# Mask or bias and row maximum in one VectorE instruction per head and block, in a two-layer transformer kernel

## The chip, the cores and the metric

The kernel runs on one core of one Trainium2 chip. The metric is the device time of one execution in microseconds (us). Five engines work side by side, each through its own queue in order: TensorE (PE, with PEld for its weight loads), VectorE (DVE), ScalarE (ACT), GpSimd (POOL) and SyncE (SP, which issues transfers).

## The reference

Two layers of different kinds run over 8 x 256 tokens of width 128, in float32. Each block is followed by a residual and a layer normalisation.

```python
x = _layernorm(x + attn0(x))   # 16 heads of 64, softmax(q k^T * scale) v, no mask
x = _layernorm(x + ffn0(x))    # tiles chosen by signatures, splines
x = _layernorm(x + attn1(x))   # linear attention gated with window attention
x = _layernorm(x + ffn1(x))    # causal attention, then 8 soft experts
```

Two of them have scores with something added to them ahead of the softmax. In the window attention, each query sees the 65 keys around it, with a learned bias per offset and head:

```python
s = einsum('bhsd,bhsd->bhs', qh, ks) * scale + rel_bias[off + WINDOW]
s = where(0 <= pos + off < S, s, -inf);  attn = softmax(s)      # 16 heads of 8
```

In the causal attention of the last block (16 heads of 64), queries and keys are normalised to length 1 first:

```python
q = l2norm(q) * q_scale;  k = l2norm(k) * k_scale
logits = where(causal, einsum('bhid,bhjd->bhij', q, k) * 10.0, NEG_INF)
attn = softmax(logits)
```

## The kernel before, in words

The tokens are cut into eight groups of 512 (two sequences each). Every group goes through five stages: A (attention without mask), B (the first feed-forward block), C (linear and window attention), D (causal attention) and E (the experts). Stages of different groups run at the same time, so that at any moment several of them share the engines.

The order of the work is not written by hand. Each piece of work is a task added by `W.add(engine, cost, function, ...)`, with a cost in nanoseconds, the buffers that it reads and writes, and a due time. `Plan.order` then makes one list out of all the tasks: it takes in turn the task that can begin first, by these costs, and counts the buffers of each class (`SLOTS`) as they are taken and given back. Tasks marked "VS" or "SV" may go to VectorE or ScalarE; the planner picks the one that would start it sooner. The queues of the engines hold the instructions in that order, whatever the chip then does. A changed cost can therefore change the order on all engines.

The scores of an attention live in two PSUM buffers of class "s" (1024 columns each), which stages A, B, C and D share. A buffer is used so:

- `scores` on TensorE writes the scores.
- `top` on VectorE adds the mask or bias, if there is one, and finds the maximum of each row, negated, into a small buffer `nmx` (class "m").
- `weigh` on ScalarE computes the exponentials out of it (L623, in stage C L1065), with `nmx` as its bias. Then the buffer is free for the next scores.

In stages A and D the function `pair` does this for two heads and one sequence of 256 tokens; there are 128 such pairs in each of the two stages. In stage A `top` is one maximum over 1024 columns (L606). In stage D the queries are cut into two halves of 128: the first half needs 128 keys, the second 256, so each head has 384 columns. There `top` adds a mask of 128x128 (`cmask`) to the two diagonal blocks of both heads (L597, 512 columns), takes the maxima (L602, two instructions), and multiplies them by the scale of the row, `rq` (L604).

Stage C works on blocks of 64 queries with 16 heads laid out as 8 slots of two heads each; a block sees 96 keys at the ends of a sequence and 128 within it. There are 64 blocks, 32 of each kind. There `top` adds `band`, the bias laid out per slot, to all 8 slots by one instruction (L1053), and takes the 8 maxima by another (L1054).

Other lines that matter below: L514 is every matrix multiplication, L651 the transposition of the weights, L636 their division by the sum on GpSimd, L520 and L522 are copies out of PSUM on ScalarE and VectorE (tasks that either may take), L536 is a step of the layer normalisation on GpSimd, L1020 prepares the queries of a block of stage C on GpSimd. Stage C takes its tiles of 512 columns from class "c", of which there are nine.

Of the kernel before, what the change touches and what calls it, by code (L numbers as in the profile page):

```python
# [12 lines left out]
ALU = mybir.AluOpType  # L13
AX = mybir.AxisListType
# [3 lines left out]
P = 128  # L18
# [13 lines left out]
NEG = -1.0e30  # L32
# [15 lines left out]
    ("k1", 256, 5),  # L48
    ("b", 512, 2),
    ("sc", 288, 1),  # L50
    ("c", 512, 9),
    ("qm", 512, 2),
    ("pbC", 512, 2),
    ("ptC", 512, 2),
# [183 lines left out]
def kernel(ctx: ExitStack, tc: tile.TileContext, a: dict, out: bass.AP):  # L238
    nc = tc.nc
# [7 lines left out]
    def ctile(name, shape, dtype=F32):  # L247
        return const.tile(shape, dtype, name=name, tag=name)
# [7 lines left out]
    W = Plan(slots)  # L256
# [171 lines left out]
    band = ctile("band", [P, WH // 2, P])  # L428
# [6 lines left out]
    def setup_c():  # L435
# [34 lines left out]
        out=hm, in_=hm, compare_op=ALU.is_ge, fill=0.0, base=0, pattern=[[-WD, WH]], channel_multiplier=1  # L470
    )
    nc.gpsimd.affine_select(
        out=hm, in_=hm, compare_op=ALU.is_ge, fill=0.0, base=WD - 1, pattern=[[WD, WH]], channel_multiplier=-1
# [14 lines left out]
    nc.gpsimd.memset(blk2, 0.0)  # L488
    nc.gpsimd.memset(blk2[:DH, 0:1], 1.0)
    nc.gpsimd.memset(blk2[DH:, 1:2], 1.0)  # L490
    cmask = ctile("cmask", [P, P])
    make_causal_mask(nc, cmask, NEG)
    ones1 = ctile("ones1", [P, 1])
    nc.gpsimd.memset(ones1, 1.0)

# [5 lines left out]
    def pe(n, cols=P, count=1, passes=2):  # L501
        return count * passes * max(0.84 * n, 0.87 * cols)

    def dve(n, count=1):
        return count * (60 + 1.05 * n)

    def scl(n, count=1):
        return count * (60 + 0.84 * n)
# [4 lines left out]
    def mm(o, lhsT, rhs, start=True, stop=True):  # L513
        nc.tensor.matmul(o, lhsT=lhsT, rhs=rhs, start=start, stop=stop)  # L514
# [3 lines left out]
    def copy(e, o, i):  # L518
        if e == "S":
            nc.scalar.copy(o, i)  # L520
        else:
            nc.vector.tensor_copy(o, i)  # L522

    def layernorm(o, z, name, after=()):

# [42 lines left out]
    def pair(pi, qT, kT, v, ov, causal, rq):  # L568

        chain = chain_d if causal else chain_a
        ncol = 3 * P if causal else 4 * P


        col = {0: (2 * P, P), 1: (0, 2 * P)} if causal else {0: (0, 2 * P), 1: (2 * P, 2 * P)}
        sps = W.buf("s", "sps")
        nmx, sums = W.buf("m", "nmx"), W.buf("m", "sums")
        S2 = "p (a k) -> p a k"

        def scores():
            q, k, s = qT("p (i t) -> p i t", t=S), kT("p (i t) -> p i t", t=S), sps(S2, a=2)
            for qc in range(2):
                c0, nk = col[qc]

                for par in range(2):
                    r = slice(par * DH, (par + 1) * DH)
                    mm(s[:, par, c0 : c0 + nk], q[r, pi, qc * P : (qc + 1) * P], k[r, pi, :nk])

        W.add("P", pe(ncol, cols=0), scores, r=[qT, kT], w=[sps, chain[0]], mode="r")  # L590

        def top():
            s = sps(S2, a=2)
            n = nmx(n=4, pattern="p (a b) -> p a b", a=2)
            if causal:
                diag = s[:, :, P : 3 * P].rearrange("p a (b k) -> p a b k", k=P)
                nc.vector.tensor_tensor(  # L597
                    out=diag, in0=diag, in1=cmask.unsqueeze(1).unsqueeze(1).to_broadcast([P, 2, 2, P]), op=ALU.add
                )
                for qc in range(2):  # L600
                    c0, nk = col[qc]
                    nc.vector.tensor_reduce(n[:, :, qc], s[:, :, c0 : c0 + nk], AX.X, ALU.max, negate=True)  # L602
                rqp = rq("p (b h) -> p h b", n=8, b=2)[:, 2 * pi : 2 * pi + 2, :]
                nc.vector.tensor_tensor(out=n, in0=n, in1=rqp, op=ALU.mult)  # L604
            else:
                nc.vector.tensor_reduce(n, s.rearrange("p a (b k) -> p a b k", k=S), AX.X, ALU.max, negate=True)  # L606

        cost = 1790 if causal else dve(1024)
        W.add("V", cost, top, r=[rq] if causal else [], w=[sps, nmx])

        pts = []
        for par in range(2):
            pb, pt = W.buf("pb", "pb"), W.buf("pt", "pt")
            sm = (sums, par)

            def weigh(par=par, pb=pb):
                s = sps(S2, a=2)
                for qc in range(2):
                    c0, nk = col[qc]
                    kw = {}  # L620
                    if causal:
                        kw["scale"] = rq()[:, qc * 4 + 2 * pi + par : qc * 4 + 2 * pi + par + 1]
                    act(  # L623
                        pb()[:, c0 : c0 + nk], s[:, par, c0 : c0 + nk], AF.Exp,
                        bias=nmx()[:, 2 * par + qc : 2 * par + qc + 1],
                        accum_out=sums()[:, 2 * par + qc : 2 * par + qc + 1], **kw,
                    )

            W.add("S", 976 if causal else 900, weigh, r=[nmx, (sps, par)] + ([rq] if causal else []), w=[pb, sm], table="exp")
            W.add("V", 73, lambda par=par: nc.vector.reciprocal(sums()[:, 2 * par : 2 * par + 2], sums()[:, 2 * par : 2 * par + 2]), w=[sm])  # L630

            def norm(e, par=par, pb=pb):
                for qc in range(2):
                    c0, nk = col[qc]
                    eng = nc.gpsimd if e == "G" else nc.vector
                    eng.tensor_scalar(  # L636
                        pb()[:, c0 : c0 + nk], pb()[:, c0 : c0 + nk],
                        sums()[:, 2 * par + qc : 2 * par + qc + 1], 1.0, ALU.mult, ALU.mult,
                    )

            W.add("G", (802 if causal else 910,), lambda norm=norm: norm("G"), r=[sm], w=[pb])
            tps = W.buf("p", "tps")

            def turn(pb=pb, tps=tps):

                at = 0
                for kc in range(2):
                    for qc in range(2):
                        c0, nk = col[qc]
                        if kc * P < nk:  # L650
                            nc.tensor.transpose(  # L651
                                tps()[:, at * P : (at + 1) * P], pb()[:, c0 + kc * P : c0 + (kc + 1) * P], ident
                            )
                            at += 1

            W.add("P", pe(P, count=ncol // P, passes=1), turn, r=[pb], w=[tps, chain[1]], hold=[pt])
            W.add("VS", (dve(ncol), scl(ncol)), lambda e, pt=pt, tps=tps: copy(e, pt()[:, :ncol], tps()[:, :ncol]), r=[tps], w=[pt])
            pts.append(pt)
        ops = W.buf("p", "ops")

        def values():
            vv = v("p (k n) -> p k n", k=2)
            for kc in range(2):
                q0 = P if causal and kc else 0
                for par in range(2):
                    hc = slice((2 * pi + par) * DH, (2 * pi + par + 1) * DH)
                    mm(
                        ops()[par * DH : (par + 1) * DH, q0:S],
                        vv[:, kc, hc],
                        pts[par]()[:, kc * S : kc * S + S - q0],  # L670
                        start=kc == 0,
                        stop=kc == 1,
                    )

        W.add("P", pe(ncol, cols=0), values, r=[v] + pts, w=[ops, chain[2]], hold=[ov], mode="c64")
        W.add("VS", (dve(256), scl(256)), lambda e: copy(e, ov(), ops()[:, :S]), r=[ops], w=[ov])

    def into_width(ovs, w, hf, o, name):
# [14 lines left out]
    def stage_a(g):  # L693
# [12 lines left out]
        def unit(b, p2):  # L706
# [31 lines left out]
            for i in range(2):  # L738
                W.at = base + (4 * b + p2 + (i + 1) / 3) / 8
                ov = W.buf("ov", "ovA")  # L740
                pair(i, qT, kT, v, ov, False, None)
                got.append(ov)
# [181 lines left out]
    def stage_c(g):  # L924
        xx = xg[g]
        V, G, A = nc.vector, nc.gpsimd, nc.scalar
# [46 lines left out]
        for b in range(2):  # L973
# [37 lines left out]
            for i, (w0, w1_) in enumerate(win_of):  # L1011
                W.at = base + 0.1 + 0.4 * b + 0.09 * i
                nk = w1_ - w0
                t0 = w0 - (QC * i - HALF)
                c0 = b * S + QC * i
# [23 lines left out]
                sps = W.buf("s", "spsC")  # L1039
# [9 lines left out]
                nmx = W.buf("m", "nmxC")  # L1049

                def top(sps=sps, nmx=nmx, nk=nk, t0=t0):
                    s8 = sps("p (u k) -> p u k", u=8)[:, :, :nk]
                    V.tensor_tensor(out=s8, in0=s8, in1=band[:, :, t0 : t0 + nk], op=ALU.add)  # L1053
                    V.tensor_reduce(nmx()[:, :8], s8, AX.X, ALU.max, negate=True)  # L1054

                W.add("V", 130 + 2 * dve(8 * nk), top, w=[sps, nmx])
                pts = []
                for half in range(2):
                    pb, pt, tps = W.buf("pbC", "pbC"), W.buf("ptC", "ptC"), W.buf("p", "tpsC")
# [318 lines left out]
```

## Time and profile before

| | |
|---|---|
| median of 3 runs | 2264.16 us (2259.54 to 2265.47) |
| profiled execution | 2259.16 us, its span 2257.3 us |
| TensorE busy | 2126.6 us, 94% of the span |
| VectorE busy | 1711.4 us, 76% |
| ScalarE busy | 1316.0 us, 58% |
| GpSimd busy | 801.7 us, 36% |
| granted TensorE clock, mean | 0.982 of full speed |

A line of the groups reads: line, engine, operation, what it writes <- what it reads, their shapes and count, then busy time in us and the mean of one in ns, then the idle time of that engine just before these instructions and who ended it. A line of the waits reads: who waited for whom, us in total, times, longest. A line of the timeline reads: start, length, instruction. The records of neighbouring instructions on one engine can overlap, so the distance between two starts is what an instruction costs its queue.

### The profile page before, as it was taken

What the parts mean: (1) busy time and instruction counts of PE and PEld (TensorE: products, weight loads), DVE (VectorE), ACT (ScalarE), POOL (GpSimd) and SP (SyncE); (2) the same over time, 40 slices, a digit from 0 to 9 for tenths busy, and PEclk for the clock granted to TensorE, in tenths of its full rate; (3) what the DMA queues carried; (4) which work ended last, traced back from release to release, by engine and by line L of the source; (5) the groups of instructions that cost most, each with busy time, mean ns of one, the idle gap of its engine ahead of it and who ended that gap; (6) DMA issues with size and microseconds to landing.
All of it is one profiled execution on the core that took longest, in us unless ns stands there. A gap on an engine that the chain in (4) does not pass through costs nothing.

```text
span 2257.3 us, 50085 instructions
## 1 busy us (share of the span) xinstructions
PE 2126.6 (94%) x18474; PEld 1611.8 (71%) x18474; DVE 1711.4 (76%) x5167; ACT 1316.0 (58%) x3824; POOL 801.7 (36%) x1441
## 2 busy tenths in 40 slices
PE   6999999999999999999999999999899989989987
PEld 5777767777777677776777767777667767767755
DVE  4789898888678977688767897588876976785741
ACT  3556656666466656565565666565565645654642
POOL 6435352444143531335213352143521441330421
PEclk8999999999999999999999999999999999999998
DMA  6100000000100001100010000100011001001101
GB/s 149 24 1 2 2 1 1 2 2 20 43 16 11 2 15 38 34 1 2 15 47 20 2 1 25 48 11 2 1 38 39 7 19 37 22 7 51 29 20 42
DMA packets 61029, 47.98 MB, mean 21 GB/s; under 512 B 4609, under 2 KB 51297, under 8 KB 60785
## 3 DMA queue, kind: packets, MB, share of 16 engines
q1 hardware_dynamic: 59200, 43.09, 6.8%
q8 instruction: 146, 2.39, 0.5%
q0 software_dynamic: 1008, 0.65, 0.3%
q10 hardware_dynamic: 576, 1.05, 0.2%
q14 instruction: 99, 0.80, 0.1%
HBM read 41.89 MB, written 2.88 MB: 20 GB/s over the span
## 4 chain that ended last, share of the span: by engine, by line
PE 31%; DVE 16%; ACT 3%; issue 2%; POOL 1%; POOLq 0%; DVEq 0%; ACTq 0%
PE p L514 25%; PE p L651 2%; PE s L514 2%; DVE m L602 2%; DVE s L597 1%; ACT pb L623 1%; DVE m L606 1%; DVE m L531 1%; POOL pb L636 1%; DVE s L1053 1%; DVE m L1054 1%; PE p L1071 1%; DVE m L1147 1%; DVE pt L522 1%; DVE m L1149 1%
## 5 line engine op out<-in xcount | busy, mean ns | idle before, releaser
L636 POOL TENSOR_SCALAR pb<-pb,m 128x256 f32<-128x256 f32 (+1 forms) x1024 | 452.4, 458 | 710.6 <-DVE m L630 611.2
L1309 ACT ACTIVATE hid<-p,b 128x512 f32<-128x512 f32 x256 | 169.3, 688 | 285.3 <-PE p L514 283.8
L651 PE MATMUL p<-ident,pb 128*128 128x128 f32 x1792 | 293.8, 284 | 22.4 <-POOL pb L636 17.0
L623 ACT ACTIVATE pb<-s,m 128x256 f32<-128x256 f32 x512 | 239.0, 488 | 112.5 <-DVE m L606 100.9
L623 ACT ACTIVATE pb<-s,m,m 128x128 f32<-128x128 f32 (+1 forms) x512 | 257.7, 525 | 62.3 <-DVE m L604 47.7
L651 PEld LDWEIGHTS p<-ident,pb 128*128 128x128 f32 x1792 | 208.1, 143 | 113.6 <-POOL pb L636 66.0
L514 PE MATMUL p<-h,we 128*128 128x512 f32 x512 | 251.5, 624 | 2.9 <-ACT hid L1309 2.5
L514 PEld LDWEIGHTS p<-we,hid 128*128 128x128 f32 x2048 | 238.6, 192 | 15.6 <-issue 10.0
L514 PE MATMUL p<-we,hid 128*128 128x128 f32 x2048 | 246.9, 276 | 1.0 <-ACT hid L1309 0.7
L520 ACT COPY pt<-p 128x384 f32<-128x384 f32 (+1 forms) x316 | 168.9, 541 | 122.6 <-PE p L651 115.7
L1217 POOL TENSOR_TENSOR kn<-kn,m 128x512 f32<-128x512 f32 x64 | 67.2, 1050 | 361.9 <-DVE m L630 224.0
L606 DVE TENSOR_REDUCE m<-s 128x4 f32<-128x1024 f32 x128 | 154.7, 1214 | 32.9 <-PE s L514 32.6
L514 PEld LDWEIGHTS p<-h,we 128*128 128x128 f32 x512 | 93.3, 197 | 98.9 <-issue 63.7
L1324 DVE SCALAR_TENSOR_TENSOR e<-p,m,e 128x128 f32<-128x128 f32 x256 | 71.7, 343 | 111.8 <-PE p L514 89.7
L514 PE MATMUL s<-ua,ua 64*128 64x256 f32 x1024 | 141.9, 401 | 10.9 <-ACT pb L623 10.8
L1065 ACT ACTIVATE pbC<-s,m 128x96 f32<-128x96 f32 (+1 forms) x512 | 135.1, 382 | 16.3 <-DVE m L1054 14.1
L514 PE MATMUL s<-ud,ud 64*128 64x128 f32 (+1 forms) x1024 | 115.7, 347 | 26.1 <-ACT pb L623 25.7
L522 DVE COPY pt<-p 128x512 f32<-128x512 f32 (+1 forms) x196 | 121.1, 623 | 22.1 <-PE p L651 19.9
L514 PE MATMUL p<-pt,ua 128*64 128x256 f32 x1024 | 136.8, 389 | 0.7 <-ACT pt L520 0.7
L602 DVE TENSOR_REDUCE m<-s 128x2 f32<-128x256 f32 (+1 forms) x256 | 130.8, 552 | 4.8
L514 PE MATMUL p<-pt,ud 128*64 128x256 f32 (+1 forms) x1024 | 117.7, 341 | 4.8 <-DVE pt L522 2.6
L514 PEld LDWEIGHTS s<-ua,ua 64*128 64x128 f32 x1024 | 92.0, 189 | 41.7 <-ACT pb L623 19.9
(298 smaller groups left out, 4420.3 us busy)
## 6 DMA issues: line engine op xcount, KB each, us to landing
we<-in_L_ffn_w_dram SPq DMA_DIRECT2D x128, 256.0 KB, 2.7
x<-_attn_hidden_states_dram SPq DMA_DIRECT2D x8, 256.0 KB, 5.3
out_dram<-x SPq DMA_DIRECT2D x8, 256.0 KB, 2.2
dpad<-k SPq DMA_DIRECT2D x1, 768.0 KB, 9.4
wq<-in_L_attn_Wq_dram ACTq DMA_DIRECT2D x2, 256.0 KB
wkv<-in_L_attn_Wkv_dram ACTq DMA_DIRECT2D x2, 256.0 KB, 7.3
wkv<-in_L_attn_Wkv_dram SPq DMA_DIRECT2D x2, 256.0 KB, 7.1
wo<-in_L_attn_Wo_dram SPq DMA_DIRECT2D x1, 512.0 KB, 11.2
```

Of the source, the lines that this page charges most:

```text
L514: nc.tensor.matmul(o, lhsT=lhsT, rhs=rhs, start=start, stop=stop)
L520: nc.scalar.copy(o, i)
L522: nc.vector.tensor_copy(o, i)
L602: nc.vector.tensor_reduce(n[:, :, qc], s[:, :, c0 : c0 + nk], AX.X, ALU.max, negate=True)
L606: nc.vector.tensor_reduce(n, s.rearrange("p a (b k) -> p a b k", k=S), AX.X, ALU.max, negate=True)
L623: act(pb()[:, c0 : c0 + nk], s[:, par, c0 : c0 + nk], AF.Exp, bias=nmx()[:, 2 * par + qc : 2 * par + qc + 1], accum_out=sums()[:, 2 * par ...
L636: eng.tensor_scalar(pb()[:, c0 : c0 + nk], pb()[:, c0 : c0 + nk], sums()[:, 2 * par + qc : 2 * par + qc + 1], 1.0, ALU.mult, ALU.mult,)
L651: nc.tensor.transpose(tps()[:, at * P : (at + 1) * P], pb()[:, c0 + kc * P : c0 + (kc + 1) * P], ident)
L1065: act(pb("p (u k) -> p u k", u=4)[:, u, :nk], s8[:, hp, :nk], AF.Exp, bias=nmx()[:, hp : hp + 1])
L1217: lambda: G.tensor_tensor(out=kn("p (h d) -> p h d", d=DH), in0=kn("p (h d) -> p h d", d=DH), in1=rqk()[:, 8:16].unsqueeze(2).to_broadcast ...
L1309: W.add("S", 571, lambda ph=ph, hid=hid, ec=ec: act(hid(), ph(), AF.Gelu_apprx_tanh, bias=b1[:, ec : ec + 1]), r=[ph], w=[hid], table="gel ...
L1324: V.scalar_tensor_tensor(m, pe_()[:, j * D : (j + 1) * D], gate()[:, j * NE + e_ : j * NE + e_ + 1], m, ALU.mult, ALU.add)
```

## The change

The addition and the maximum become one instruction, `tensor_tensor_reduce`, which writes the sum back into the scores and the maximum of the row into a column of its own (`masked_max`). It works on one row per partition, so there is one for each head and query half in stage D (four per pair) and one for each of the 8 slots in stage C. The maximum comes out positive: in stage D the sign is taken along in the multiplication by `rq`, in stage C one more small instruction turns it. For the second query half, the mask must cover 256 keys, so `cmask` grows to 256 columns, the first 128 of them zero. The costs that the planner is told change with it, and class "c" has one buffer less.

```diff
-    ("c", 512, 9),
+    ("c", 512, 8),
...
-    cmask = ctile("cmask", [P, P])
-    make_causal_mask(nc, cmask, NEG)
+
+    cmask = ctile("cmask", [P, 2 * P])
+    nc.gpsimd.memset(cmask[:, :P], 0.0)
+    make_causal_mask(nc, cmask[:, P:], NEG)
...
+    def masked_max(s, m, mx):
+
+        nc.vector.tensor_tensor_reduce(
+            out=s, in0=s, in1=m, scale=1.0, scalar=-3.0e38, op0=ALU.add, op1=ALU.max, accum_out=mx
+        )
...
             if causal:
-                diag = s[:, :, P : 3 * P].rearrange("p a (b k) -> p a b k", k=P)
-                nc.vector.tensor_tensor(
-                    out=diag, in0=diag, in1=cmask.unsqueeze(1).unsqueeze(1).to_broadcast([P, 2, 2, P]), op=ALU.add
-                )
-                for qc in range(2):
-                    c0, nk = col[qc]
-                    nc.vector.tensor_reduce(n[:, :, qc], s[:, :, c0 : c0 + nk], AX.X, ALU.max, negate=True)
+                for par in range(2):
+                    for qc in range(2):
+                        c0, nk = col[qc]
+                        sv = s[:, par, c0 : c0 + nk]
+                        masked_max(sv, cmask[:, 2 * P - nk :], n[:, par, qc : qc + 1])
                 rqp = rq("p (b h) -> p h b", n=8, b=2)[:, 2 * pi : 2 * pi + 2, :]
-                nc.vector.tensor_tensor(out=n, in0=n, in1=rqp, op=ALU.mult)
+                nc.vector.scalar_tensor_tensor(n, n, -1.0, rqp, ALU.mult, ALU.mult)
...
-        cost = 1790 if causal else dve(1024)
+        cost = 1200 if causal else dve(1024)
...
                     s8 = sps("p (u k) -> p u k", u=8)[:, :, :nk]
-                    V.tensor_tensor(out=s8, in0=s8, in1=band[:, :, t0 : t0 + nk], op=ALU.add)
-                    V.tensor_reduce(nmx()[:, :8], s8, AX.X, ALU.max, negate=True)
-
-                W.add("V", 130 + 2 * dve(8 * nk), top, w=[sps, nmx])
+                    for u in range(8):
+                        masked_max(s8[:, u, :], band[:, u, t0 : t0 + nk], nmx()[:, u : u + 1])
+                    V.tensor_scalar(nmx()[:, :8], nmx()[:, :8], -1.0, None, ALU.mult)
+
+                W.add("V", 70 + 8 * dve(nk), top, w=[sps, nmx])
```

`dve(n)` is 60 + 1.05 n ns, the planner's cost of one VectorE instruction over n columns.

## The prediction, as it was made

> **What bounds the kernel now.** I read the page first (busy shares, then the chain that ended last), then the waits, then VectorE's groups with their shapes kept apart, then the timeline of VectorE in a crowded stretch.
>
> ```profile
> PE 2126.6 (94%) x18474; PEld 1611.8 (71%) x18474; DVE 1711.4 (76%) x5167; ACT 1316.0 (58%) x3824; POOL 801.7 (36%) x1441
> ```
>
> TensorE is busy nearly throughout, VectorE three quarters of the time. The chain says how much of the end each one sets:
>
> ```profile
> PE 31%; DVE 16%; ACT 3%; issue 2%; POOL 1%; POOLq 0%; DVEq 0%; ACTq 0%
> ```
>
> The chain covers 53% of the span (from about 1050 us on), and 16 of the 53 points are VectorE: 30%. So TensorE comes first, and VectorE sets the pace for almost a third. The waits (us in total, times, longest) show how they touch around the change:
>
> ```profile
> ACT pb L623 <- DVE m L606: 100.9, 42, 6.7
> ...
> PEld s L514 <- ACT pb L623: 53.2, 58, 5.7
> ...
> ACT pb L623 <- DVE m L604: 47.7, 23, 5.1
> ...
> PE s L514 <- ACT pb L623: 37.0, 29, 5.3
> ```
>
> ScalarE's exponentials wait for the row maxima that VectorE makes (L606 without mask, L604 last step of the causal one), and TensorE's next scores (s) wait 90.2 us, 87 times, until those exponentials have freed one of the two score buffers. The groups give the work that the change touches (busy us, mean ns of one):
>
> ```profile
> L597 DVE TENSOR_TENSOR s<-s,cmask 128x512 f32<-128x512 f32 x128 | 88.2, 689 | 27.7 <-PE s L514 27.1
> L602 DVE TENSOR_REDUCE m<-s 128x2 f32<-128x512 f32 x128 | 87.1, 680 | 0.0
> ...
> L602 DVE TENSOR_REDUCE m<-s 128x2 f32<-128x256 f32 x128 | 54.3, 424 | 4.8
> ...
> L1054 DVE TENSOR_REDUCE m<-s 128x8 f32<-128x1024 f32 x32 | 39.2, 1224 | 1.2
> L1053 DVE TENSOR_TENSOR s<-s,band 128x1024 f32<-128x1024 f32 x32 | 39.0, 1220 | 0.7 <-PE s L514 0.7
> ```
>
> Rows of neighbours overlap, so a sum of means overstates what the queue pays. The timeline of VectorE (start us, length us) gives the true step, from start to start:
>
> ```profile
> 688.41 0.69 DVE L597 TENSOR_TENSOR s<-s,cmask 128x512 f32<-128x512 f32 x1
> 689.13 1.02 DVE L602 TENSOR_REDUCE m<-s 128x2 f32<-128x256 f32 x2
> 690.19 0.16 DVE L604 TENSOR_TENSOR m<-m,m 128x4 f32<-128x4 f32 x1
> 690.27 1.22 DVE L606 TENSOR_REDUCE m<-s 128x4 f32<-128x1024 f32 x1
> ```
>
> One causal maximum costs 690.27 - 688.41 = **1.86 us** of VectorE. In the same way the banded one costs 1.86 us on 8x96 columns (675.29 to 677.15) and 2.39 us on 8x128 (1.25 for the add, 1.14 for the maximum). A small reciprocal at 642.73 is followed at 642.80 by the next instruction, though its row is 0.15 long: an independent instruction costs about 0.07 us beyond its elements. One that needs the result of the one before starts about 0.04 us after that one's end (L604 after L602: 690.15 to 690.19).
>
> [...] copies of 512 columns start 0.60 us apart [...]. No run here shows the new instruction. [...] VectorE's trace has none, ScalarE's has one:
>
> ```profile
> 1016.30 0.48 ACT L623 ACTIVATE pb<-s,m 128x256 f32<-128x256 f32 x1 [0.16 <-DVE m L630]
> 1016.67 0.19 ACT L623 ACTIVATION_READ_ACCUMULATOR pb<-s,m 128x1 f32 x1
> 1016.76 0.46 ACT L623 ACTIVATE pb<-s,m 128x256 f32<-128x256 f32 x1
> ```
>
> There the read starts before the main row ends and costs 0.09 us. So "one instruction per head" is probably two, and its price r decides this case.
>
> **The change, part by part.** With the read as a small instruction (r = 0.075 us), a fused instruction of N columns takes 0.00104 N + 0.075 + r: 0.25 us for 96, 0.283 for 128, 0.417 for 256. The last small instruction (sign, scale) needs the last maximum: 0.15 + 0.04 in place of 0.075 until it starts, then 0.08 for itself, 0.195 in all.
> - Causal (128 pairs): 2 x 0.283 + 2 x 0.417 + 0.195 = 1.60 against 1.86 us, 0.265 less. x128 = **-34 us**. VectorE passes over 768 columns in place of 512 + 768, and the wait between mask and maximum goes.
> - Banded, 128 columns (32 blocks): 8 x 0.283 + 0.195 = 2.46 against 2.39: +2 us. With 96 columns (32 blocks): 8 x 0.25 + 0.195 = 2.20 against 1.86: **+11 us**. Eight fixed prices eat the saved pass.
> - Sum: **-21 us** of VectorE's 1711. Bounds: at r = 0 it is 1.295, 1.86 and 1.595 us, -72 - 17 - 8 = **-98 us**; if each read had to await its main instruction ([...] then 0.04 + 0.075), it is 2.09, 3.44 and 3.17 us, **+104 us**. There are 128 x 4 + 64 x 8 = 1024 reads, so 10 ns of r are 10 us.
> - What the end sees: 30% of -21 is -6 us. The score buffers turn round faster: of 328 turns 39% are causal and 20% banded, so 87 waits x (0.39 x 0.265 - 0.2 x 0.2) give -5.5 us.
> - The planner orders all queues by its costs, and these change by more than I expect of the chip: 590 ns a pair (1790 to 1200), 775 and 506 ns a block, together 75 + 25 + 16 = 116 us against my 21. The old costs were within 0.1 us of the steps above. It will think VectorE freer and give it copies that ScalarE could do (L522 on VectorE holds some 380 us that either may take); if a third of the 116 is refilled, 39 us move over, and ScalarE, at 58%, gets that much lighter. What waits behind a late fused group is the next copy on VectorE and the exponentials of that pair, then the scores that want its buffer. I charge 4 us.
> - Stage C's buffers drop from 9 to 8: the block itself needs hT, ql, qw, kw, kl, vl, lin and winT, eight; the ninth serves the hand-over between groups, and there the next group's layernorm root on GpSimd (L536 waits 137.5 us in 29 times) comes later anyway. Zero; without that cover one projection a group waits for the gate's end, under 2 us x 7.
> - The wider mask: one more GpSimd memset of 128x128 at the start, under 1 us, beside the loads of weights that fill the first 56 us. SyncE's queue gets nothing. The causal sign joins the multiplication (same count); the banded sign is one more small instruction, counted above.
> - Sum: -6 - 5.5 + 4, about **-8 us**. The profiled execution took 2259.16 us (span 2257.3), so 2251; the median of the runs, 2264.16, is 5.0 above it, so I say **2256 us**. A measurement here can tell about 0.3% (6.8 us) from no change.
>
> **Rivals.**
> - A: the read is nearly free (r to 0.03). For: ScalarE's read overlaps the main row. Against: even the smallest VectorE instruction takes 0.07. At r = 0: 30% of -98 is -29; buffers 87 x (0.39 x 0.565 + 0.2 x 0.4) = -26; 2209 us; at r = 0.03 two thirds of that gain, some 2227.
> - B, slower: the read waits for its main instruction to end. Place: between the fused instructions of one top, so all of the queue behind it pays. From r = 0.096 on (98 / 1024) VectorE loses. At +104 us: 30% is +31, buffers 87 x (0.39 x 0.225 + 0.2 x 1.18) = +28, the planner's error, now 220 us, +8: 2331 us. For: dependent instructions here do wait for the row's end. Against: ScalarE's read doesn't.
> - C: the new order itself is worse: VectorE, wrongly thought free, takes the 39 us of copies and becomes late in the stretches where it is full (677 to 734: 49.5 of 57 us). 30% of 39 is +12, and with as much lost in waits some 2288 us. For: full stretches. Against: ScalarE is relieved.
> - D: nothing happens because TensorE alone bounds: 2264. Against: VectorE's 30% of the chain.
>
> **How the numbers follow.** My forecast 52% (own range 2230 to 2282, since any new order moves the sum by about 1%), A 23%, B 15%, C with D 10%. The forecast gives faster 0.29, same 0.10, slower 0.13; A faster 0.22, same 0.01; B slower 0.15; C and D slower 0.10. Together 0.51, 0.11, 0.38. The range 2212 to 2312 leaves out the far ends of A and B.
>
> **What would show it.** VectorE has 5167 + 128 + 64 x 7 = 5743 rows, or 6767 with reads shown. A causal top steps 1.6 us (1.3 for A, 2.1 for B), a banded one 2.2 and 2.46. Busy VectorE falls by about 20 us less what copies it takes over; L522's count on VectorE rises, L520's falls. The 90 us that scores wait for buffers fall. Wrong: reads with a step over 0.1 us, [...] or TensorE waiting on VectorE's copies more than the 130 us it idles now.

## The result, and the profile after

The changed kernel takes **2358.4 us** (median of 4 runs, 2357.6 to 2360.6) against 2261.85 us for the kernel before in the same comparison: a ratio of **1.042**, 95% interval 1.040 to 1.044. The prediction said 2256, with a range up to 2312, and faster. The change loses 96.5 us, the 96 us of what follows.

The first part of the page after (busy us, share of the span, instructions), and its chain:

```profile
PE 2169.9 (92%) x18474; PEld 1624.7 (69%) x18474; DVE 1785.2 (76%) x6834; ACT 1298.9 (55%) x3758; POOL 799.7 (34%) x1442
```

```profile
PE 53%; DVE 30%; issue 8%; ACT 4%; POOL 4%; DMA 1%; SPq 1%; POOLq 0%; DVEq 0%; ACTq 0%
```

VectorE is busy 74 us more, not 21 less. Two experiments below part these: the fused work alone makes VectorE 40 us busier (e1_old_costs), the new order alone 34 us (e2_new_costs_old_work), by tasks that move over from ScalarE. The share of the span is the same 76%, which shows how little a share says: the span grew with it. VectorE's part of the chain is also the same, 30 of about 100 points, where it was 16 of 53. The groups of VectorE, shapes apart, show the new instruction as two rows, the fused one and the read of its maximum, 1024 times each, as ScalarE's trace before has 1024 reads of its own beside the exponentials of L623:

```profile
L528 DVE DVE_READ_ACCUMULATOR2_ANT m<- 128x1 f32 x1024 | 144.2, 141 | 0.0
L528 DVE CUSTOM_DVE_ANT_0 s<-s,cmask 128x256 f32<-128x256 f32 x256 | 110.7, 432 | 9.2
L528 DVE CUSTOM_DVE_ANT_0 s<-s,band 128x128 f32<-128x128 f32 x256 | 76.3, 298 | 14.4 <-PE s L516 5.5
L528 DVE CUSTOM_DVE_ANT_0 s<-s,cmask 128x128 f32<-128x128 f32 x256 | 75.2, 294 | 19.7 <-PE s L516 14.8
...
L528 DVE CUSTOM_DVE_ANT_0 s<-s,band 128x96 f32<-128x96 f32 x256 | 67.9, 265 | 10.9 <-PE s L516 2.7
```

The fused rows last 265 ns on 96 columns, 294 and 298 on 128, and 432 on 256. What a top costs is seen in the timeline of VectorE (start us, length us), here a banded one on 96 columns (cut short) and a causal one behind it:

```profile
707.49 0.27 DVE L528 CUSTOM_DVE_ANT_0 s<-s,band 128x96 f32<-128x96 f32 x1 [0.57 <-PE s L516]
707.67 0.14 DVE L528 DVE_READ_ACCUMULATOR2_ANT m<- 128x1 f32 x1
707.85 0.27 DVE L528 CUSTOM_DVE_ANT_0 s<-s,band 128x96 f32<-128x96 f32 x1
...
710.36 0.17 DVE L1061 TENSOR_SCALAR m<-m 128x8 f32<-128x8 f32 x1
710.44 0.29 DVE L528 CUSTOM_DVE_ANT_0 s<-s,cmask 128x128 f32<-128x128 f32 x1
710.64 0.14 DVE L528 DVE_READ_ACCUMULATOR2_ANT m<- 128x1 f32 x1
710.82 0.43 DVE L528 CUSTOM_DVE_ANT_0 s<-s,cmask 128x256 f32<-128x256 f32 x1
711.17 0.14 DVE L528 DVE_READ_ACCUMULATOR2_ANT m<- 128x1 f32 x1
711.34 0.30 DVE L528 CUSTOM_DVE_ANT_0 s<-s,cmask 128x128 f32<-128x128 f32 x1
...
712.26 0.17 DVE L610 SCALAR_TENSOR_TENSOR m<-m,m 128x4 f32<-128x4 f32 x1
712.34 0.68 DVE L524 COPY pt<-p 128x512 f32<-128x512 f32 x1
```

The read begins 0.20 us after its fused instruction, while that one's row is still open: it does not wait for that row to end. But the *next* fused instruction begins 0.18 us after the read, that is 0.04 us after the read's row ends (710.64 + 0.14 = 710.78, then 710.82). So each read costs its queue 0.17 to 0.18 us (median over all 1024 reads 0.175). The causal top takes 712.34 - 710.44 = 1.90 us (before: 1.86), the banded one 2.95 us on 96 columns (707.49 to 710.44; before: 1.86) and 3.22 us on 128 (584.38 to 587.60, not shown; before: 2.39). Over all: 128 x 0.04 + 32 x 1.09 + 32 x 0.83 = 5 + 35 + 27 = **67 us more** of VectorE, where the prediction had 21 less.

Why does the next one wait? The trace lists for each instruction the semaphores that it raises and those that it waits for. All 1024 reads raise the same one, which only instructions of VectorE raise. Of the 832 fused instructions that follow another one of their top, 809 carry a wait on it, and the other 23 have that wait in an instruction of its own just ahead. The fused instruction reads a tile (the scores, in PSUM) that the one before wrote. The columns are others, but the wait is there. Of the two maxima of L602 before, the second one only reads the scores, as the first did: it had no such wait in any of the 128 pairs, and the two overlapped: it starts 0.34 us after the first, whose row is 0.42 long.

The waits show where this comes out. Line numbers have moved: the reciprocals on VectorE are L630 before and L636 after, the divisions on GpSimd L636 and then L642, the transpositions on TensorE L651 and then L657, the exponentials L623 and then L629. Before:

```profile
POOL pb L636 <- DVE m L630: 611.2, 208, 19.9
...
PEld p L651 <- POOL pb L636: 66.0, 153, 10.6
...
PE p L651 <- POOL pb L636: 17.0, 9, 10.2
```

After:

```profile
POOL pb L642 <- DVE m L636: 775.3, 231, 26.4
...
PEld p L657 <- POOL pb L642: 103.5, 195, 10.7
...
PEld s L516 <- ACT pb L629: 36.4, 48, 3.6
...
PE p L657 <- POOL pb L642: 32.1, 33, 10.3
...
PE s L516 <- ACT pb L629: 22.7, 34, 3.4
```

GpSimd's divisions wait longer for the small reciprocals on VectorE, 775 us in place of 611. TensorE's transpositions wait for the divisions, 135.6 us in place of 83.0. The wait for score buffers that I had watched did fall, from 90.2 to 59.1 us, while the time rose. The new order does that, and not a quicker top: with the new order and the old work it is 60.9 us, with the fused work in the old order 92.5 (e2_new_costs_old_work and e1_old_costs below).

TensorE stands still 56 us more (span less busy time, 130.7 us before and 186.3 after). The other 43 us of the longer span lie in its rows, 2169.9 us in place of 2126.6 for the same matrix multiplications. One part shows in the clock that the trace records: TensorE was granted half its clock for 80 us of the span before and for 129 after, a mean of 0.982 and 0.973. An estimate from these: some 48 us more at half the clock cost about 24 us at most. Whether the standing still brings the lower clock wasn't tried.

### The profile page after: what moved, and what is told of

Read it like the earlier page. It is cut to its first block, busy times and chain, and to the rows that moved or that the text cites. A ratio compares the mean times of both kernels' runs of the same rounds, so it can differ in the third digit from the quotient of the medians.

```text
span 2356.2 us, 51721 instructions
## 1 busy us (share of the span) xinstructions
PE 2169.9 (92%) x18474; PEld 1624.7 (69%) x18474; DVE 1785.2 (76%) x6834; ACT 1298.9 (55%) x3758; POOL 799.7 (34%) x1442
## 3 DMA queue, kind: packets, MB, share of 16 engines
q8 instruction: 146, 2.39, 0.4%
q10 hardware_dynamic: 576, 1.05, 0.2%
## 4 chain that ended last, share of the span: by engine, by line
PE 53%; DVE 30%; issue 8%; ACT 4%; POOL 4%; DMA 1%; SPq 1%; POOLq 0%; DVEq 0%; ACTq 0%
PE p L516 39%; DVE s L528 9%; PE s L516 6%; PE p L657 5%; ACT pb L629 2%; POOL pb L642 2%; DVE m L528 2%; DVE m L612 2%; PE p L1078 1%; DVE x L552 1%; DVE m L539 1%; DVE pt L524 1%; DVE m L1155 1%; DVE m L1156 1%; DVE m L1189 1%
## 5 line engine op out<-in xcount | busy, mean ns | idle before, releaser
L642 POOL TENSOR_SCALAR pb<-pb,m 128x256 f32<-128x256 f32 (+1 forms) x1024 | 451.7, 458 | 878.5 <-DVE m L636 775.3
L657 PE MATMUL p<-ident,pb 128*128 128x128 f32 x1792 | 308.5, 289 | 52.7 <-POOL pb L642 32.1
L629 ACT ACTIVATE pb<-s,m,m 128x128 f32<-128x128 f32 (+1 forms) x512 | 258.0, 521 | 159.5 <-DVE m L610 135.1
L657 PEld LDWEIGHTS p<-ident,pb 128*128 128x128 f32 x1792 | 210.6, 145 | 153.0 <-POOL pb L642 103.5
L629 ACT ACTIVATE pb<-s,m 128x256 f32<-128x256 f32 x512 | 238.7, 488 | 95.9 <-DVE m L612 82.4
L522 ACT COPY pt<-p 128x384 f32<-128x384 f32 (+1 forms) x319 | 169.0, 540 | 142.9 <-PE p L657 131.3
L528 DVE CUSTOM_DVE_ANT_0 s<-s,cmask 128x128 f32<-128x128 f32 (+1 forms) x512 | 185.9, 363 | 28.8 <-PE s L516 14.8
L528 DVE CUSTOM_DVE_ANT_0 s<-s,band 128x96 f32<-128x96 f32 (+1 forms) x512 | 144.1, 282 | 25.3 <-PE s L516 8.2
L524 DVE COPY pt<-p 128x512 f32<-128x512 f32 (+1 forms) x193 | 119.4, 621 | 33.6 <-PE p L657 32.5
L528 DVE DVE_READ_ACCUMULATOR2_ANT m<- 128x1 f32 x1024 | 144.2, 141 | 0.0
```

What stands on the lines that cost most here:

```text
L528: nc.vector.tensor_tensor_reduce(out=s, in0=s, in1=m, scale=1.0, scalar=-3.0e38, op0=ALU.add, op1=ALU.max, accum_out=mx)
L629: act(pb()[:, c0 : c0 + nk], s[:, par, c0 : c0 + nk], AF.Exp, bias=nmx()[:, 2 * par + qc : 2 * par + qc + 1], accum_out=sums()[:, 2 * par ...
L642: eng.tensor_scalar(pb()[:, c0 : c0 + nk], pb()[:, c0 : c0 + nk], sums()[:, 2 * par + qc : 2 * par + qc + 1], 1.0, ALU.mult, ALU.mult,)
L657: nc.tensor.transpose(tps()[:, at * P : (at + 1) * P], pb()[:, c0 + kc * P : c0 + (kc + 1) * P], ident)
```

## The experiments

The questions: how much of the 96 us is the fused work, how much the new order; what makes the read dear; and whether the fused form can be had without that. Two theories to start with: **W**, the fused work is dearer on VectorE; **O**, the order hurts, because its costs promise 116 us that aren't there.

### Work and order apart

The changed instructions, with the old costs told to the planner. The lists of TensorE and ScalarE are then those of the kernel before, task by task, though class "c" has 8 buffers.

```diff
-        cost = 1200 if causal else dve(1024)
+        cost = 1790 if causal else dve(1024)
-                W.add("V", 70 + 8 * dve(nk), top, w=[sps, nmx])
+                W.add("V", 130 + 2 * dve(8 * nk), top, w=[sps, nmx])
```

> The changed instructions in the order of before: the planner is told the old costs (1790 a pair; 130 + 2 dve(8 nk) a block), so TensorE's, ScalarE's and VectorE's tasks come in the order of before, and class c has 8 buffers, which moves nothing. Theory W (the fused work itself is dearer on VectorE, 1.90 us a causal top, 2.95 and some 3.2 us a banded one, 67 us in all): most of the 96 us stay, 2335 to 2350 us. Theory O (the new order, made from costs that promise 116 us less, is what hurts): most is gone, 2275 to 2295 us.

Measured: 2313.7 us against 2262.2, ratio 1.022 (1.020 to 1.024). Neither range: the work alone loses 51 us, about half of it all.

The reverse edit in the kernel before: its own instructions, the new costs.

```diff
-        cost = 1790 if causal else dve(1024)
+        cost = 1200 if causal else dve(1024)
-                W.add("V", 130 + 2 * dve(8 * nk), top, w=[sps, nmx])
+                W.add("V", 70 + 8 * dve(nk), top, w=[sps, nmx])
```

> The instructions of before in the order of after: only the two costs told to the planner are the new ones. TensorE and ScalarE have exactly the order of after. Theory W: 2262 to 2275 us. Theory O: 2330 to 2350 us. If both parts count and add up, this and e1_old_costs together give the 96 us: for example 2285 here and 2335 there.

Measured: 2287.9 us, ratio 1.011 (1.009 to 1.012), in neither theory's range. The order alone loses 26 us. 51 + 26 = 77; the other 19 us come only when dear work meets the wrong order. Both theories hold in part.

Stage D alone fused, in the old order:

```diff
-                    for u in range(8):
-                        masked_max(s8[:, u, :], band[:, u, t0 : t0 + nk], nmx()[:, u : u + 1])
-                    V.tensor_scalar(nmx()[:, :8], nmx()[:, :8], -1.0, None, ALU.mult)
+                    V.tensor_tensor(out=s8, in0=s8, in1=band[:, :, t0 : t0 + nk], op=ALU.add)
+                    V.tensor_reduce(nmx()[:, :8], s8, AX.X, ALU.max, negate=True)
```

> Fused instructions in stage D alone, stage C with its two passes, everything in the order of before. W: a causal top steps 1.90 us in place of 1.86, 128 x 0.04 = 5 us of VectorE, so 2262 to 2270 us, and the cost of the change lies in the banded tops (62 of the 67 us). A rival to W, that every fused instruction disturbs by more than its step [...], would give about half of what e1_old_costs loses, 2295 to 2310.

Measured: 2273.1 us, ratio 1.0044 (1.0027 to 1.0061), 3 us above the expected range and far from the rival's. Of the 51 us of the work, 11 belong to stage D and, by difference, some 40 to stage C with its eight reads per block; stage C alone was not run. Why 5 us of VectorE cost 11 in stage D stays open.

### The wait

As the first experiment (old order), but the sum goes to a scratch tile of three parts, used in turn:

```diff
+    scr = ctile("scr", [P, 3 * P])
...
-            out=s, in0=s, in1=m,
+            out=scr[:, k0 : k0 + s.shape[-1]], in0=s, in1=m,
```

> As e1_old_costs, but the fused instruction writes its sum into a scratch tile of three parts instead of back into the scores, so no fused instruction reads a tile that the one before wrote, and none must await the accumulator read before it. Mask and bias are therefore left out of the exponentials (not out of the maxima). If the wait is what makes r 0.175 us, the read steps 0.07 to 0.08 us, a causal top 1.6 us, a banded one 2.2 and 2.46 as in the prediction, VectorE's work is 21 us below before and the time is 2245 to 2265 us. If the read itself holds what follows (the engine, not the wait), the steps stay 0.175 and the time stays with e1_old_costs.

Measured: **2240.6 us**, ratio 0.990 (0.989 to 0.992). Its timeline:

```profile
642.80 0.27 DVE L530 CUSTOM_DVE_ANT_0 scr<-s,cmask 128x128 f32<-128x128 f32 x1
643.00 0.08 DVE L530 DVE_READ_ACCUMULATOR2_ANT m<- 128x1 f32 x1
643.00 0.41 DVE L530 CUSTOM_DVE_ANT_0 scr<-s,cmask 128x256 f32<-128x256 f32 x1
643.35 0.07 DVE L530 DVE_READ_ACCUMULATOR2_ANT m<- 128x1 f32 x1
643.35 0.28 DVE L530 CUSTOM_DVE_ANT_0 scr<-s,cmask 128x128 f32<-128x128 f32 x1
...
644.01 0.16 DVE L612 SCALAR_TENSOR_TENSOR m<-m,m 128x4 f32<-128x4 f32 x1
644.10 0.42 DVE L524 COPY ov<-p 128x256 f32<-128x256 f32 x1
```

The next fused instruction begins together with the read (643.00 and 643.00): the read's step is zero. A causal top takes 644.10 - 642.80 = 1.30 us, a banded one 1.63 and 1.88: 128 x 0.56 + 32 x 0.23 + 32 x 0.51 = 95 us less than before. That was the lower bound of the prediction (98). Both the step and the time came out below what was expected.

In this trace 562 of the 832 fused instructions that follow another one still carry a wait on VectorE's own semaphore. It can't be for the read just ahead, since all 562 start together with that read; by the edit it is for the instruction two or three back, which wrote the same part. So it isn't a wait as such that takes time here, but one for the read just ahead.

Two things had changed at once, the wait and the place of the output. So the same again with the scratch in SBUF, but always the same columns, which brings the wait back:

```diff
-            out=scr[:, k0 : k0 + s.shape[-1]], in0=s, in1=m,
+            out=scr[:, : s.shape[-1]], in0=s, in1=m,
```

> As e6_no_wait (order of before, sum to a scratch tile in SBUF, mask and bias left out of the exponentials), but always to the same columns, so each fused instruction must again wait for the one before it, while its output lies in SBUF. If the wait itself costs the 0.17 us a read: a causal top steps 1.9 us and the time is that of e1_old_costs, 2300 to 2317. If it was writing back to the PSUM tile that made the read dear: it stays with e6_no_wait, 2237 to 2250.

Measured: 2273.2 us, ratio 1.0045 (1.0029 to 1.0061), between the two ranges. The timeline tells why:

```profile
644.19 0.28 DVE L530 CUSTOM_DVE_ANT_0 scr<-s,cmask 128x128 f32<-128x128 f32 x1
644.40 0.09 DVE L530 DVE_READ_ACCUMULATOR2_ANT m<- 128x1 f32 x1
644.52 0.42 DVE L530 CUSTOM_DVE_ANT_0 scr<-s,cmask 128x256 f32<-128x256 f32 x1
644.87 0.08 DVE L530 DVE_READ_ACCUMULATOR2_ANT m<- 128x1 f32 x1
644.98 0.29 DVE L530 CUSTOM_DVE_ANT_0 scr<-s,cmask 128x128 f32<-128x128 f32 x1
```

With the wait the read steps 0.11 to 0.12 us here (median 0.117), and the row of the read is 0.08 us; in the changed kernel, with the sum in PSUM, the row is 0.14 us and the step 0.17 to 0.18. So the price has two parts: without a wait nothing, with a wait 0.115, and 0.06 more for the longer read when the sum goes back to PSUM. Only the wait makes either count. In the time, from no wait to the wait is 33 us here, from there to the sum in PSUM another 40.

### The costs told to the planner

The changed kernel as it is, with the costs that the chip shows:

```diff
-        cost = 1200 if causal else dve(1024)
+        cost = 1910 if causal else dve(1024)
-                W.add("V", 70 + 8 * dve(nk), top, w=[sps, nmx])
+                W.add("V", 80 + 8 * (258 + 1.05 * nk), top, w=[sps, nmx])
```

> The changed instructions as they are, the planner told what they take on the chip: 1910 ns a causal top, 2950 and 3220 a banded one. Theory M (the new order hurts because its costs are wrong for the work): the order made with true costs is at least as good as the order of before, so 2300 to 2325 us, that is e1_old_costs or better, and 35 us or more below the change. Theory L (any other order than the one of before loses some 25 us, right costs or not): 2330 to 2350.

Measured: **2278.1 us**, ratio 1.0057 (1.0033 to 1.0080). Same instructions, 80 us less than the change, and 36 less than in the old order. This is beyond what theory M asked for. The groups show part of the way: the copies that either engine may take (L522 before, L524 after, all shapes summed) hold 381 us of VectorE before, 410 in the change, and 351 here. Told too little, the planner puts 29 us of copies more on VectorE than before; told the truth, it leaves 58 us fewer there than in the change.

The change with its own order and costs, without the wait (the scratch tile of three parts again):

> The change with its own order and costs, only that the sum goes to the scratch tile of three parts, so that no fused instruction waits for the read before it (mask and bias are left out of the exponentials, not of the maxima). The costs told are then nearly true (1200 for 1.30 us, 1356 and 1625 for 1.62 and 1.88). Theory M: no order penalty is left, 2225 to 2250 us, as e6_no_wait or better. Theory L: e6_no_wait plus 25, 2260 to 2275.

Measured: **2213.3 us**, ratio 0.978 (0.976 to 0.979), below both ranges. The same order that loses 26 us with the old work is the best of all with the work for which its costs are nearly true, copies on VectorE at 411 us included. So the order isn't bad; it is made for a VectorE that the wait takes away. In this order the wait and the sum in PSUM together cost 2358 - 2213 = 145 us, in the old order 2314 - 2241 = 73; the two were parted in the old order alone.

How far does a new order with right costs move the time by itself? The kernel before, with the cost of a causal top at 1860:

> The kernel before with nothing changed but the cost told for a causal top, 1860 in place of 1790 ns, which is what it takes on the chip. It measures how far a new order made with right costs moves the time by itself. If the order of before has no special luck: 2255 to 2270 us. If any other order loses some 25 us, as in e2_new_costs_old_work: 2280 to 2295.

Measured: 2252.4 us, ratio 0.995 (0.993 to 0.997), just below both ranges. A correction of 70 ns gives 13 us. With the 26 us the other way above, this is the scale on which one order differs from another here, and the order of before has no special luck.

### Versions that keep the result

The sum written to SBUF, stage D alone: into the buffers `pb`, where the exponentials then work in place.

```diff
+        pbs = [W.buf("pb", "pb") for _ in range(2)] if causal else None
...
-            out=s, in0=s, in1=m,
+            out=o, in0=s, in1=m,
...
-        cost = 1200 if causal else dve(1024)
-        W.add("V", cost, top, r=[rq] if causal else [], w=[sps, nmx])
+        cost = 1400 if causal else dve(1024)
+        W.add("V", cost, top, r=[rq, sps] if causal else [], w=[nmx, *pbs] if causal else [sps, nmx])
```

> Stage D alone fused, and its sum written to the SBUF buffers pb, where the exponentials then work in place; stage C keeps its two passes and old cost. No fused instruction reads what another wrote, so a causal top should step 1.30 us (1.86 before), 72 us less of VectorE, and the score buffer is free before the exponentials. Cost told 1400. Both pb buffers of a pair are taken earlier, and ScalarE reads SBUF in place of PSUM. If the wait was the whole trouble: 2240 to 2258 us. If the earlier hold of pb costs as much as the wait: 2262 to 2285.

Measured: **2233.8 us**, ratio 0.986 (0.983 to 0.988), below both expected ranges. This run has an order of its own, so that the 32 us it gains against before hold the saved work and the new order together; they weren't parted. The causal top is that of the scratch experiment:

```profile
662.48 0.28 DVE L528 CUSTOM_DVE_ANT_0 pb<-s,cmask 128x128 f32<-128x128 f32 x1
662.68 0.08 DVE L528 DVE_READ_ACCUMULATOR2_ANT m<- 128x1 f32 x1
662.68 0.42 DVE L528 CUSTOM_DVE_ANT_0 pb<-s,cmask 128x256 f32<-128x256 f32 x1
```

Both stages so, `pb` in D and `pbC` in C:

> Both stages fused with their sums written to SBUF (pb in stage D, pbC in stage C), nothing left out of the result, costs told 1300 and 200 + 8 (75 + 1.05 nk). Tops of 1.30, 1.62 and 1.88 us, VectorE about 98 us below before. If waits are the whole trouble: 2225 to 2250 us, as e6_no_wait. If stage C suffers because both pbC buffers are now held from the top on: 2255 to 2290.

Measured: 2234.0 us, ratio 0.986 (0.984 to 0.988). It beats both kernels too, but stage C's part, some 24 us of VectorE, brings nothing that shows. VectorE isn't less busy either, 1651.7 us against 1649.6 with stage D alone: in this run's order its copies rise from 378 to 400 us, which ScalarE is spared. Whether the early hold of both `pbC` buffers costs something besides wasn't tried.

The other way: leave the wait and fill it. Each fused instruction becomes a task of its own, so that the planner can place other work between.

```diff
+                    W.add("V", 75 + 1.05 * col[qc][1], part, w=[sps, nmx])
+        cost = 80 if causal else dve(1024)
...
+                    W.add("V", 75 + 1.05 * nk, part, w=[sps, nmx])
+                W.add("V", 80, top, w=[sps, nmx])
```

> The change with nothing left out and the sum written in place, but each fused instruction is a task of its own (75 + 1.05 n ns), and the last small one too. They stay in order within a top and still wait for one another, but the planner, which puts 80 ns between dependent tasks of one engine, may place other VectorE work, fused instructions of another top among it, in between. If the wait costs only when nothing else fills it: reads step near 0 where another instruction follows, and 2215 to 2245 us. If a wait costs its time whatever is placed between: 2300 to 2360.

Measured: 2298.1 us, ratio 1.015 (1.012 to 1.017): 60 us better than the change, far from the range expected of free filling and 2 us below the other. Where the gap is filled, the read is free even with the sum in PSUM:

```profile
705.54 0.43 DVE L528 CUSTOM_DVE_ANT_0 s<-s,cmask 128x256 f32<-128x256 f32 x1
705.89 0.14 DVE L528 DVE_READ_ACCUMULATOR2_ANT m<- 128x1 f32 x1
705.89 0.55 DVE L1113 RECIPROCAL m<-p 128x64 f32<-128x64 f32 x1
```

So 632 of the 1024 reads step at most 0.025 us, but 374 still step 0.16 us or more. And a top now lasts longer: from the start of its first instruction to that of its last a causal one takes 2.67 us (median) where it took 1.82 in the change, and TensorE waits 102.7 us for score buffers in place of 59.1. Stage D alone in this way:

> As e12_split_tasks for stage D, with stage C in its two passes and old cost. If filled waits are free: 72 of the 98 us of VectorE are still saved, 2225 to 2250 us. If not: 2265 to 2285, as e4_causal_only.

Measured: 2269.1 us, ratio 1.0025 (1.0012 to 1.0038), in the second range: 4 us above before, where the unsplit one was 11 above. Here 268 of 512 reads step at most 0.025 us and 230 still 0.16 us or more, so that only about half of the waits were filled. How much of the gain the longer tops take back stays open.

## Why the prediction was wrong

- **The step that failed is the fused instruction's price**, "0.00104 N + 0.075 + r" with r = 0.075. The first two terms held, and the traces show them: before, copies that follow one another step 0.334 us on 256 columns, 0.465 on 384 and 0.598 on 512 (medians), 0.00103 us a column and 0.07 beside; without the wait the fused instructions step 0.18 us on 96 columns, 0.21 on 128 and 0.35 on 256 (e6_no_wait). The read's r was mis-sized in the case that the kernel makes: 0.17 to 0.18 us, above the break-even of 0.096 that the text gave, and hence slower: 67 us more of VectorE, which alone, in the old order, cost 51 us. I had asked what the read costs, and not which of the four or eight instructions of a top depends on which. I even read off L604 what a dependence costs (0.04 us after the other's end; median of the 128: 0.035), and took the fused ones as independent, like the maxima of L602. These only read the scores; the fused ones read *and write* them.
- **The sum**, -34 + 2 + 11 = -21 us, came out as +5 + 27 + 35 = +67. Rival B had the right place (between the fused instructions of one top), sign and point of decision. Its mechanism was the wrong way round: the read doesn't wait for its main instruction (it starts 0.22 us after it, at the median of the 1024, always inside its row); the next main instruction waits for the read (it starts 0.034 us after the read's row). Its 104 us rested on my estimate of the fused rows, which no run had shown; with the rows that the trace after shows (0.265 us on 96 columns, 0.298 and 0.294 on 128, 0.432 on 256, each with 0.04 + 0.075 behind it) the same sum would be 111. Either is too much (67), and its 8 us for the planner's error were too few; that its 2331 us come within 27 of the result owes something to luck, as the two errors partly cancel. Rival A's bound was what the chip does without the wait: read free, 95 us less. The 0.07 us that the text held against it is what small instructions step in the trace before (the reciprocals of L630 with no idle time behind them 0.072 us at the median, 0.049 at the least), but not what the read does.
- **Two instructions in place of one**, as the prediction concluded from ScalarE's trace: right. The trace after has 1024 rows of each.
- **"I charge 4 us" for the planner** was the second failure. The order alone costs 26 us, with the dear instructions 80 against an order made with true costs. I had computed that its costs promise 95 us more than I expected, and the move of copies: 39 us predicted, 29 measured. I priced that with a guess. Rival C had this mechanism, and its 2288 us are what the new order with the old work took (2287.9); so close a hit is partly luck, as its 39 us of copies were 29. What it left out are the 19 us that come when the order meets the dear work, since I thought of it apart from B.
- **"What the end sees: 30%"** was too little for added work and too much for saved work. In the old order, the 67 us added to VectorE cost 51 at the end, 77%, and the 95 us saved gave 22, 23%. No single share holds for both.
- **The score buffers** (-5.5 us) were not where the time went; in the old order, with the fused work, that wait is about the 90 us of before (92.5). TensorE's wait for the divisions rose there from 83.0 to 98.1 us, and in the change to 135.6.
- **Nothing for the ninth buffer of class "c"**: right. With the old costs, the order with eight is the same on TensorE and ScalarE, task by task.
- **Rows**: 6767 were expected with reads shown, 6834 are there. The other 67 are tasks that moved from ScalarE; e1_old_costs, with the old order, has the 6767.

## What to carry to other kernels

Before pricing a fused instruction by its length, list which instruction in a row reads a tile that the one before wrote. Here, writing back in place into a PSUM tile made a chain out of instructions on different columns, each waiting for the read of the one before to end (0.175 us a read). With the result in separate parts of another tile, the same instructions overlapped (rows of 0.28 us on 128 columns, steps of 0.21). Whether an update in place in an SBUF tile makes the same chain wasn't run; in the scratch tile, writes to separate parts of one SBUF tile made none (reads stepped 0). When a planner orders the queues, the costs told to it are part of the change: they were wrong by 0.7 us for a causal top and 1.6 us for a banded one, and the same instructions with true costs got back 80 of the 96 us.

## What the runs showed of the hardware

The read of the accumulator on VectorE took no step of its own: where the next instruction didn't wait for it, that one started at the same recorded time, whether it was another fused one (e6_no_wait, 643.00 and 643.00) or a reciprocal (e12_split_tasks, 705.89 and 705.89). Its row was 0.08 us where the fused instruction wrote to SBUF and 0.14 us where it wrote to PSUM, and this counted only for an instruction that waited for it, which started about 0.035 us after the row's end: 0.117 us after the read's start in the one case (e11_wait_in_sbuf) and 0.175 us in the other (the changed kernel; medians). The fused rows themselves hardly differed (284 ns to SBUF in e6_no_wait, 294 ns to PSUM in the changed kernel, 128 columns).
